# Attention scores on 64 array rows instead of 32 in the mixer of a four-layer network, with its second q and k projected midway

## The chip, the cores and the metric

The kernel runs on one core of a Trainium2 chip. The metric is the device time of one execution in microseconds (us), the median of several runs. Before the change it is 6611.78 us, the median of three runs (6609.2, 6611.78 and 6629.58 us). The profile is of one further execution, whose span is 6630.4 us.

## The reference

Eight images of 256 channels and 32 x 32 = 1024 positions go through four residual layers, each fed by a group norm of the current x. Everything is float32.

```python
x = x + _L0_conv_ref(_gn(x), ...)   # attention over 1024 positions, 8 heads of 64
x = x + _L1_conv_ref(_gn(x), ...)   # 3x3 convolution
x = x + _L2_conv_ref(_gn(x), ...)   # 3x3 convolution
x = x + _L3_conv_ref(_gn(x), ...)   # selective scans, gates, then a mixer, then a 3x3 depthwise step
```

The change is in layer 3, in the part that the code calls the mixer. Its input is xm2, 1024 positions of 256 channels:

```python
x_local = conv1d(xm2.transpose(0, 2, 1), lc_w, lc_b, groups=Cc, pad=1).transpose(0, 2, 1)
x_global = mha(xm2, attn_inw, attn_inb, attn_outw, attn_outb)   # 8 heads of 32
x_out = jnp.concatenate([x_local, x_global], axis=-1) @ fc_w.T + fc_b
...
att = jax.nn.softmax(q @ k.transpose(0, 1, 3, 2) * (1.0 / hd ** 0.5), axis=-1)   # hd = 32
```

## The kernel before

**Stages of an image.** front_attention is layer 0 and front_convs are layers 1 and 2. scan_layers holds the norms and the selective scans of layer 3 in four branches. back_layers holds the gates, the projections and the mixer; back_out and back_end hold the projections, norms and the depthwise convolution behind it, up to the output.

**Order of the work.** Everything is written out without loops on the chip. For each image b, interleave (line 1335) mixes two streams. The dense stream has the back layers of image b-1 (its mixer is in it), then the front of image b+1. The other stream is the scans of image b. Each piece of the dense stream yields a cost; a step of the scans is placed each time the sum of the costs has grown by PACE (line 1364: 1.8 for the first image, 2.95 for the middle ones, 1.6 for the last). So the places of the scans among the dense instructions follow from the yielded costs alone. Each engine runs its own queue in order, and an instruction that waits holds up all that is behind it. In the mixer of image 6 the scans of image 7 run alongside and no front follows; the mixer of image 7 runs with nothing beside it.

**Scans.** A unit of scans goes drive (GpSimd multiplies du by bc into hs, line 931), decays (ScalarE, da), scan (VectorE, hs), weigh (GpSimd, line 963) and add_up (TensorE sums into y, four matmuls at once with sel, 128 rows by 32 columns).

**The mixer** (mixer_attention, line 1044). v is projected for all heads. Then q and k are projected, 256 channels each, as two tiles of 128 channels for each: a tile holds four heads of 32 rows. All four projections come before the attention, in the order q of heads 0 to 3, k of heads 0 to 3, q of heads 4 to 7, k of heads 4 to 7. The evacuation from the PSUM adds the bias and, for q, multiplies by 32^-0.5, on VectorE.

**The attention loop** (attention) is shared by the front and the mixer. It takes pairs of heads. A unit is one pair, one half of the 1024 queries and one block of 128 keys; there are 64 units. A unit's scores are two matmuls, one for each head, into the two halves of one 1024-column PSUM tile, big, of which there are two; k is the stationary operand. ScalarE takes the exponential of it into p. Two units later, values multiplies p by v, again two matmuls, each with 128 rows and 64 columns, into acc. In the front a head has 64 channels, so the two scores of a pair use array rows 0 to 63 and 64 to 127. In the mixer a head has 32, so they use two neighbouring strips of 32 rows (0 and 32, or 64 and 96). A float32 matmul shows as two instructions in the profile, so the scores of a unit are four and the values four.

A pair's tensors are asked for 8 units before its first unit (pair_of(units[n + 8]["t"])). When a pair is done, take copies acc out, and DMAs carry the outputs and the sums of the exponentials to o and to a DRAM tile; after the second pair of a q tile, invert divides by the sums.

**Shared tiles.** work() gives tiles of 128 x 1026 from a pool of 12 (tp). q, k, o, p, x2 (the mixer's input), local and most other temporaries of the dense stream come from it, and each waits until one is free.

**local.** Before mixer_attention starts, back_layers computes x_local for both channel tiles (depthwise3: one ScalarE and two VectorE operations for each). The loop around the mixer counts its yields; at the 58th it makes the first statistics and the norm of the next image's front (next(begin)).

The engine proxies (line 101) issue nearly all instructions, so nearly all groups of the profile have line 101 and are told apart by their tiles: big<-qk,qk are the mixer's scores, big<-q,k the front's, acc<-p,v the values of both.

Of the kernel before, what the change touches and what calls it, by code (L numbers as in the profile page):

```python
# [19 lines left out]
P = 128  # L20
# [13 lines left out]
def preact_stack(ctx: ExitStack, tc: tile.TileContext, I, out, cols):  # L34
# [28 lines left out]
    def work(name):  # L63
        return tp.tile([P, TP], F32, tag="t", name=name)
# [4 lines left out]
    def big_tile():  # L69
        return ps_big.tile([P, N], F32, tag="big", name="big")  # L70
# [142 lines left out]
    vector.tensor_scalar_mul(qdw, qdw, 2.0)  # L213
    half_d = wp.tile([P, NB], F32, name="half_d")
    vector.tensor_scalar_mul(half_d, vec[:, cols["mD"] : cols["mD"] + NB], 0.5)
    half_qb = wp.tile([P, 2], F32, name="half_qb")
    vector.tensor_scalar_mul(
        half_qb, vec[:, cols["qpwb"] : cols["qpwb"] + 2], 0.5
# [140 lines left out]
    def inner(t):  # L359
        return t[:, 1 : N + 1]  # L360
# [683 lines left out]
    def mixer_attention(x2, img, exact=False):  # L1044


        v = vp.tile([P, NKT, 8, 64], F32, tag="v", name="v3")
        vector.memset(v[:, :, :, 32:64], 1.0)
        wv = chunk("ainv", 0)
        for kt in range(0, NKT, 4):  # L1050
            ps = big_tile()
            for i in range(4):
                for c in range(2):
                    tensor.matmul(
                        ps[:, i * C : (i + 1) * C],
                        inner(x2[c])[:, (kt + i) * P : (kt + i + 1) * P],
                        wv[:, c],
                        start=c == 0,
                        stop=c == 1,
                    )  # L1060
            vector.tensor_copy(
                v[:, kt : kt + 4, :, 0:32],
                ps.rearrange("p (k a b) -> p k a b", k=4, b=32),
            )
            yield 3.8

        qk = {}
        for t in (0, 2, 1, 3):
            qk[t] = work("qk3")
            w = chunk("ainqk", t)  # L1070
            ps = big_tile()
            for h in range(2):
                for c in range(2):
                    tensor.matmul(
                        ps[:, HALVES[h]],
                        w[:, c],
                        inner(x2[c])[:, HALVES[h]],
                        start=c == 0,
                        stop=c == 1,
                    )  # L1080
            scale = 32.0**-0.5 if t < 2 else 1.0
            vector.tensor_scalar(
                qk[t][:, 0:N], ps, col("ain_b", t), scale, ALU.add, ALU.mult
            )
            yield 3.4

        o = img["o3"] = [work("o3_0"), work("o3_1")]

        def head(i):
            t, rows = i // 4, slice((i % 4) * 32, (i % 4) * 32 + 32)  # L1090

            def take(half, acc):

                vector.tensor_scalar_add(
                    o[t][rows, half], acc, col("ain_b", 4 + t, rows)
                )

            return {
                "q": qk[t][rows, 0:N],
                "k": qk[2 + t][rows, 0:N],  # L1100
                "v": lambda kt: v[:, kt, i, 0:32],
                "rows": rows,
                "take": take,
            }

        if exact:
            attention_exact(head(i) for i in range(8))
            return

        sums = {}  # L1110

        def pair(i):
            t = i // 4
            rows = [slice((j % 4) * 32, (j % 4) * 32 + 32) for j in (i, i + 1)]

            def v_of(j):
                return lambda kt: v[:, kt, j]

            def take(h, acc, _):
                if t not in sums:  # L1120
                    sums[t] = dp.tile([4, N], F32, tag="sums4", name="sums")
                both = half_work("both")
                scalar.copy(both, acc)
                for e in range(2):
                    j, at = (i + e) % 4, e * 64
                    nc.sync.dma_start(
                        out=o[t][rows[e], HALVES[h]], in_=both[at : at + 32]
                    )
                    nc.sync.dma_start(
                        out=sums[t][j : j + 1, HALVES[h]],  # L1130
                        in_=both[at + 32 : at + 33],
                    )
                if i % 4 == 2 and h == 1:
                    ot = o[t][:, 0:N]

                    def finish(r):
                        vector.tensor_mul(ot, ot, r)
                        vector.tensor_scalar_add(ot, ot, col("ain_b", 4 + t))

                    return invert(sums[t], 4, 32, finish)  # L1140

            return {
                "q": [qk[t][r, 0:N] for r in rows],
                "k": [qk[2 + t][r, 0:N] for r in rows],
                "v": [v_of(i), v_of(i + 1)],
                "take": take,
            }

        yield from attention([lambda i=i: pair(i) for i in range(0, 8, 2)], False)

    def back_layers(img, exact=False, begin=None):

# [64 lines left out]
        for t in x2:  # L1217
            zero_ends(t)

        def evac_x2(m, ps):  # L1220
            vector.scalar_tensor_tensor(
                inner(x2[m]), ps, col("fpw_b", m), inner(xs[m]), ALU.add, ALU.add
            )

        yield from project("fpw", fd, evac_x2)


        local = [work("local0"), work("local1")]
        for t in range(2):
            depthwise3(local[t][:, 0:N], x2[t], "lc_w", "lc_b", t)  # L1230
        for n, cost in enumerate(mixer_attention(x2, img, exact)):
            yield cost
            if n == 58 and begin is not None:
                next(begin)
        img["mix"] = xt, local

    def back_out(img):
# [89 lines left out]
    def drain(*streams):  # L1327
        for s in streams:
            for _ in s:
                pass  # L1330
# [200 lines left out]
```

## Time and profile before

| What | Value |
|---|---|
| Median of 3 runs | 6611.78 us |
| Span of the profiled execution | 6630.4 us |
| TensorE (PE) busy | 5708.6 us, 86% |
| VectorE (DVE) busy | 3903.6 us, 59% |
| ScalarE (ACT) busy | 2687.2 us, 41% |
| GpSimd (POOL) busy | 2684.8 us, 40% |
| Mean granted TensorE clock | 0.892 of full |
| Mixer's scores, big<-qk,qk, 32 rows, 2048 instructions | 658.2 us busy |
| Front's scores, big<-q,k, 64 rows, 2048 instructions | 602.5 us busy |
| Values of both, acc<-p,v, 4096 instructions | 1189.7 us busy |
| Mixer of image 0 to 5, first score to last | 181.7 to 191.0 us |
| Mixer of image 6 (beside the last scans), mixer of image 7 (alone) | 349.7 us, 130.1 us |

A group's line in the profile reads: line, engine, operation, the tiles out<-in with their shapes, the count; then busy microseconds and mean nanoseconds of one; then idle time of the engine just before, and what ended most of it. Matmuls overlap, so the mean of one is longer than busy time divided by the count. PEclk is the clock granted to TensorE as a share of full speed[...]. "Chain" is the chain of waits that ended last. The seven mixers with scans beside them are longer than the one that runs alone.

### The profile page before, as it was taken

The page shows a single profiled execution, that of the slowest core. Times are in us where ns is not written, and L with a number is a line of the kernel's source. Part 1 is how long each engine was busy: PE and PEld are TensorE (multiplying, and loading weights), DVE is VectorE, ACT ScalarE, POOL GpSimd, SP SyncE. Part 2 cuts the span into 40 slices and gives each one's busy share as a digit, 9 for nine tenths or more (in the row PEclk, how much of TensorE's full clock was granted, in tenths as well). Part 3 has the DMA queues.
Part 4 walks back from the last instruction along what each step waited for, and adds up shares of the span by engine and source line. Part 5 has one row for each costly group of instructions (what it writes and reads, how often), then busy time and mean ns, then how long its engine had stood idle before and what let it go on. Part 6 is the DMA issues. An engine that isn't in the chain of part 4 may idle for free.

```text
span 6630.4 us, 52730 instructions
## 1 busy us (share of the span) xinstructions
PE 5708.6 (86%) x17602; PEld 1926.6 (29%) x17602; DVE 3903.6 (59%) x4613; ACT 2687.2 (41%) x3225; POOL 2684.8 (40%) x1295
## 2 busy tenths in 40 slices
PE   8887689897998979998899989999799988978596
PEld 2331133222422234222332223222342223311222
DVE  4248745577465775567655675557755676455522
ACT  4134424553254532544245432555235442344242
POOL 0016662634355251642526334462526426176300
PEclk9988888998998989899999989899899999867697
DMA  1022332322233122331223222241213212233200
GB/s 41 27 60 79 77 90 73 101 60 65 74 97 91 48 69 76 88 83 52 76 78 92 70 64 80 72 110 45 79 59 105 79 53 80 65 94 89 58 21 26
DMA packets 217969, 471.36 MB, mean 71 GB/s; under 512 B 60244, under 2 KB 103636, under 8 KB 215640
## 3 DMA queue, kind: packets, MB, share of 16 engines
q1 hardware_dynamic: 217688, 467.90, 25.4%
q8 instruction: 141, 2.31, 0.1%
q14 instruction: 140, 1.15, 0.1%
HBM read 395.36 MB, written 63.96 MB: 69 GB/s over the span
## 4 chain that ended last, share of the span: by engine, by line
PE 53%; DVE 25%; DMA 6%; issue 6%; ACT 5%; POOL 4%; SPq 1%; POOLq 0%; DVEq 0%; ACTq 0%
PE big L101 34%; PE acc L101 12%; DVE hs L101 5%; PE da L101 4%; DVE p L101 3%; PE y L101 2%; DVE u L101 2%; DVE dw L101 2%; POOL hs L963 2%; POOL hs L931 2%; DVE t L101 1%; DVE dt L101 1%; DMA du_m<-a 1%; DVE st L101 1%; ACT p L101 1%
## 5 line engine op out<-in xcount | busy, mean ns | idle before, releaser
L931 POOL TENSOR_TENSOR hs<-du,bc 128x1024 f32<-128x1024 f32 x512 | 1319.8, 2594 | 1912.6 <-DMA du<-du_m 767.4
L963 POOL TENSOR_TENSOR hs<-hs,bc 128x1024 f32<-128x1024 f32 x512 | 1278.8, 2498 | 693.2 <-DVE hs L101 480.4
L101 ACT ACTIVATE p<-big 128x1024 f32<-128x1024 f32 x1024 | 1036.1, 1019 | 769.3 <-PE big L101 764.8
L101 PE MATMUL acc<-p,v 128*64 128x512 f32 x4096 | 1189.7, 653 | 2.6 <-ACT o L101 2.6
L101 PE MATMUL big<-im,w 128*128 128x512 f32 x2304 | 1073.7, 622 | 120.9 <-ACT im L101 102.6
L101 ACT ACTIVATE da<-dt,a_neg 128x512 f32<-128x512 f32 x1024 | 688.7, 687 | 791.3 <-DVE hs L101 484.3
L101 DVE TENSOR_TENSOR p<-p 128x1024 f32<-128x1024 f32 x448 | 717.0, 1600 | 273.7 <-ACT p L101 183.9
L101 DVE TENSOR_TENSOR_SCAN hs<-da,carry,hs 128x512 f32<-128x512 f32 x512 | 628.2, 1268 | 382.8 <-POOL hs L931 301.2
L101 DVE TENSOR_TENSOR_SCAN hs<-da,hs 128x512 f32<-128x512 f32 x512 | 600.0, 1207 | 256.8 <-ACT da L101 166.3
L101 PE MATMUL big<-q,k 64*128 64x512 f32 x2048 | 602.5, 657 | 76.7 <-ACT p L101 47.8
L101 PE MATMUL big<-qk,qk 32*128 32x512 f32 x2048 | 658.2, 687 | 9.2 <-ACT p L101 6.5
L101 PEld LDWEIGHTS big<-im,w 128*128 128x128 f32 x2304 | 445.4, 198 | 752.0 <-issue 613.8
L101 PE MATMUL y<-hs,sel 128*32 128x512 f32 x2048 | 410.9, 676 | 210.9 <-POOL hs L963 180.8
L962 POOL COPY carry<-hs 128x2 f32<-128x2 f32 x256 | 97.5, 381 | 947.6 <-DVE hs L101 928.2
L101 PEld LDWEIGHTS acc<-p,v 128*64 128x64 f32 x4096 | 217.6, 140 | 843.2 <-issue 759.8
L101 PEld LDWEIGHTS big<-qk,qk 32*128 32x128 f32 x2048 | 173.8, 195 | 487.2 <-issue 269.2
L101 PEld LDWEIGHTS big<-q,k 64*128 64x128 f32 x2048 | 161.2, 188 | 503.0 <-issue 247.4
L101 PE MATMUL big<-o,w 128*128 128x512 f32 x384 | 196.2, 664 | 92.6 <-DVE o L101 92.6
L101 PE MATMUL big<-xn,w 128*128 128x512 f32 x512 | 232.4, 608 | 5.6 <-ACT p L101 5.6
L101 DVE SCALAR_TENSOR_TENSOR dw<-xo,vec,dw 128x961 f32<-128x961 f32 (+1 forms) x128 | 194.1, 1550 | 29.3 <-ACT dw L101 29.1
L101 DVE SCALAR_TENSOR_TENSOR u<-raw,vec,u 128x1024 f32<-128x1024 f32 x96 | 153.9, 1603 | 87.2 <-ACT u L101 86.7
L101 DVE SCALAR_TENSOR_TENSOR xt<-big,vec,xt 128x1024 f32<-128x1024 f32 x48 | 61.4, 1279 | 236.2 <-PE big L101 236.2
(191 smaller groups left out, 5231.1 us busy)
## 6 DMA issues: line engine op xcount, KB each, us to landing
bc<-bc SPq DMA_DIRECT2D x1024, 128.0 KB
dt<-dt_m SPq DMA_DIRECT2D x512, 128.0 KB
du<-du_m SPq DMA_DIRECT2D x512, 128.0 KB
w<-in_wc SPq DMA_DIRECT2D x192, 192.0 KB
rs<-inv SPq DMA_DIRECT2D x64, 256.0 KB
dt_m<-dt SPq DMA_DIRECT2D x64, 256.0 KB
du_m<-a SPq DMA_DIRECT2D x64, 256.0 KB
xt<-in_x SPq DMA_DIRECT2D x8, 1024.0 KB
```

The lines of the kernel that those rows point to most:

```text
L101: made = issue(*args, **kwargs)
L931: nc.gpsimd.tensor_mul(u["hs"], u["du"], both_groups(u["bc"][:, 0]))
L962: nc.gpsimd.tensor_copy(carry[:, u["q"], g : g + 2], hs[:, :, HALF - 1])
L963: nc.gpsimd.tensor_mul(hs, hs, both_groups(u["bc"][:, 1]))
```

## The change

Each head's scores are to use 64 rows of the array. The pair becomes heads i and i + 2 of one q tile, which lie in different halves of the 128 rows. k is taken in those halves, 64 rows with the channels of two heads. So that the second head in the half adds nothing, q is kept twice: once with heads 1 and 3 set to zero, once with heads 0 and 2. A column of factors, alt, that is 32^-0.5 or 0 by strips of 32 rows makes both in the evacuation: VectorE makes the first, ScalarE the second, with a bias that is already multiplied (alt_b). This is the arrangement in which the array sees as many rows as in the front.

Two more things move. A second q takes more of the shared tiles, so q and k of heads 4 to 7 are projected when their first pair is asked for (unit 24), in a drain that yields no cost to the pace of the scans, and no longer ahead of the attention. And local is computed midway, after the 34th and the 40th yield, instead of before; the norm of the next front stays at the same unit (yield 56 instead of 58, as two yields are gone). The branch marked exact is adapted; it runs only when the sums are out of range.

```diff
+    alt = wp.tile([P, 2], F32, name="alt")
+    nc.gpsimd.memset(alt, 0.0)
+    for g in range(4):
+        nc.gpsimd.memset(alt[g * 32 : g * 32 + 32, g % 2 : g % 2 + 1], 32.0**-0.5)
+    alt_b = wp.tile([P, 2, 2], F32, name="alt_b")
+    for t in range(2):
+        vector.tensor_scalar_mul(alt_b[:, t], alt, col("ain_b", t))
...
         qk = {}
-        for t in (0, 2, 1, 3):
-            qk[t] = work("qk3")
-            w = chunk("ainqk", t)
-            ps = big_tile()
...
-            scale = 32.0**-0.5 if t < 2 else 1.0
-            vector.tensor_scalar(
-                qk[t][:, 0:N], ps, col("ain_b", t), scale, ALU.add, ALU.mult
-            )
-            yield 3.4
+
+        def q_and_k(t):
+            for at in (t, 2 + t):
+                w = chunk("ainqk", at)
+                ps = big_tile()
...
+                if at == t:
+                    q = [work("qk3")[:, 0:N] for _ in range(2)]
+                    vector.tensor_scalar(
+                        q[0], ps, col("ain_b", t), alt[:, 0:1], ALU.add, ALU.mult
+                    )
+                    scalar.activation(
+                        q[1], ps, AF.Identity, bias=alt_b[:, t, 1:2], scale=alt[:, 1:2]
+                    )
+                else:
+                    k = work("qk3")[:, 0:N]
+                    vector.tensor_scalar_add(k, ps, col("ain_b", at))
+                yield 3.4
+            qk[t] = q, k
+
+        yield from q_and_k(0)
...
         def pair(i):
             t = i // 4
-            rows = [slice((j % 4) * 32, (j % 4) * 32 + 32) for j in (i, i + 1)]
+            if t not in qk:
+                drain(q_and_k(t))
+            q, k = qk[t][0][i % 2], qk[t][1]
...
                 for e in range(2):
-                    j, at = (i + e) % 4, e * 64
+                    j, at = i % 4 + 2 * e, e * 64
...
-                if i % 4 == 2 and h == 1:
+                if i % 4 == 1 and h == 1:
...
             return {
-                "q": [qk[t][r, 0:N] for r in rows],
-                "k": [qk[2 + t][r, 0:N] for r in rows],
-                "v": [v_of(i), v_of(i + 1)],
+                "q": [q[e * 64 : e * 64 + 64] for e in range(2)],
+                "k": [k[e * 64 : e * 64 + 64] for e in range(2)],
+                "v": [v_of(i), v_of(i + 2)],
                 "take": take,
             }
 
-        yield from attention([lambda i=i: pair(i) for i in range(0, 8, 2)], False)
+        yield from attention([lambda i=i: pair(i) for i in (0, 1, 4, 5)], False)
...
-        local = [work("local0"), work("local1")]
-        for t in range(2):
+        local = []
+
+        def add_local():
+            t = len(local)
+            local.append(work("local"))
             depthwise3(local[t][:, 0:N], x2[t], "lc_w", "lc_b", t)
+
         for n, cost in enumerate(mixer_attention(x2, img, exact)):
             yield cost
-            if n == 58 and begin is not None:
+            if n in (34, 40):
+                add_local()
+            if n == 56 and begin is not None:
                 next(begin)
+        while len(local) < 2:
+            add_local()
         img["mix"] = xt, local
```

More of the change, by code (lines that the diff above doesn't have):

```diff
@@ L1067, in mixer_attention @@
         qk = {}
-        for t in (0, 2, 1, 3):
-            qk[t] = work("qk3")
-            w = chunk("ainqk", t)
-            ps = big_tile()
[L1072 to L1079, printed above, removed]
-                    )
-            scale = 32.0**-0.5 if t < 2 else 1.0
-            vector.tensor_scalar(
-                qk[t][:, 0:N], ps, col("ain_b", t), scale, ALU.add, ALU.mult
-            )
-            yield 3.4
+        def q_and_k(t):
+            for at in (t, 2 + t):
+                w = chunk("ainqk", at)
+                ps = big_tile()
+                for h in range(2):
+                    for c in range(2):
+                        tensor.matmul(
+                            ps[:, HALVES[h]],
+                            w[:, c],
+                            inner(x2[c])[:, HALVES[h]],
+                            start=c == 0,
+                            stop=c == 1,
+                        )
[3 more added lines that the diff above has]
+                        q[0], ps, col("ain_b", t), alt[:, 0:1], ALU.add, ALU.mult
+                    )
+                    scalar.activation(
[7 more added lines that the diff above has]
+        yield from q_and_k(0)
         o = img["o3"] = [work("o3_0"), work("o3_1")]
@@ L1096, in take @@
                 )
+            if t not in qk:
+                drain(q_and_k(t))
             return {
-                "q": qk[t][rows, 0:N],
-                "k": qk[2 + t][rows, 0:N],
+                "q": qk[t][0][i % 2][rows],
+                "k": qk[t][1][rows],
                 "v": lambda kt: v[:, kt, i, 0:32],
@@ L1113, in pair @@
             t = i // 4
-            rows = [slice((j % 4) * 32, (j % 4) * 32 + 32) for j in (i, i + 1)]
+            if t not in qk:
+                drain(q_and_k(t))
+            q, k = qk[t][0][i % 2], qk[t][1]
             def v_of(j):
@@ L1124, in take @@
                 for e in range(2):
-                    j, at = (i + e) % 4, e * 64
+                    j, at = i % 4 + 2 * e, e * 64
                     nc.sync.dma_start(
-                        out=o[t][rows[e], HALVES[h]], in_=both[at : at + 32]
+                        out=o[t][j * 32 : j * 32 + 32, HALVES[h]],
+                        in_=both[at : at + 32],
                     )
```

## The prediction

> **What bounds the kernel now.** I read the page first: which engine is busiest, at what clock it ran, and which chain ended last.
>
> ```profile
> PE 5708.6 (86%) x17602; PEld 1926.6 (29%) x17602; DVE 3903.6 (59%) x4613; ACT 2687.2 (41%) x3225; POOL 2684.8 (40%) x1295
> ...
> PEclk9988888998998989899999989899899999867697
> ...
> PE 53%; DVE 25%; DMA 6%; issue 6%; ACT 5%; POOL 4%; SPq 1%; POOLq 0%; DVEq 0%; ACTq 0%
> ```
>
> TensorE is busy 86% of the span and holds 53% of the chain; its clock is not always full (mean 0.892 in the view of cores). So a TensorE microsecond counts, and so does the clock at which it is spent. Next, the groups of instructions that the change touches, from the page:
>
> ```profile
> L101 PE MATMUL acc<-p,v 128*64 128x512 f32 x4096 | 1189.7, 653 | 2.6 <-ACT o L101 2.6
> ...
> L101 PE MATMUL big<-q,k 64*128 64x512 f32 x2048 | 602.5, 657 | 76.7 <-ACT p L101 47.8
> L101 PE MATMUL big<-qk,qk 32*128 32x512 f32 x2048 | 658.2, 687 | 9.2 <-ACT p L101 6.5
> ```
>
> The front attention scores with 64 rows (q,k), the mixer with 32 (qk,qk), with the same number of instructions. The mixer's cost 56 us more. Is a 32-row pair slower in itself? The timeline of TensorE in undisturbed stretches, mixer of the last image, then front of the first (start, us, what):
>
> ```profile
> 6420.72 1.13 PE L101 MATMUL big<-qk,qk 32*128 32x512 f32 x4
> 6421.77 1.08 PE L101 MATMUL acc<-p,v 128*64 128x512 f32 x4
> 6422.78 1.13 PE L101 MATMUL big<-qk,qk 32*128 32x512 f32 x4
> ```
> ```profile
> 164.58 1.13 PE L101 MATMUL big<-q,k 64*128 64x512 f32 x4
> 165.64 1.08 PE L101 MATMUL acc<-p,v 128*64 128x512 f32 x4
> 166.65 1.13 PE L101 MATMUL big<-q,k 64*128 64x512 f32 x4
> ```
>
> No: one unit of scores and values takes 2.06 to 2.07 us in both. The difference is the clock. Windows over whole stages (mixers of images 1, 6 and 7, then the front of image 3; stretch, length, PE busy, PEclk, DMA share, GB/s):
>
> ```profile
> 1868.20:2058.10 189.90, 173.92 (x625) 0.90 0.35 92
> 5759.50:6109.20 349.70, 279.19 (x737) 0.72 0.32 84
> 6366.70:6496.80 130.10, 129.78 (x505) 1.00 0.05 13
> 2124.00:2301.30 177.30, 170.66 (x629) 0.99 0.21 56
> ```
>
> The trace's clock is only ever 1.00 or 0.50 and changes on a grid of 3.413 us. Windows on that grid, three in the mixer of image 6, two in the front of image 1:
>
> ```profile
> 5771.51:5774.93 3.42, 3.42 (x10) 0.50 0.20 52
> 5774.93:5778.34 3.41, 3.41 (x8) 0.50 0.27 102
> 5778.34:5781.75 3.41, 3.41 (x10) 0.50 0.00 0
> 487.73:491.14 3.41, 3.41 (x6) 0.50 0.02 4
> 491.14:494.55 3.41, 3.41 (x16) 1.00 0.27 73
> ```
>
> Both times TensorE is fully busy at half clock. In the front one such window brings the full clock back; in the mixer it stays at half for ten windows (5764.7 to 5798.8). I counted this over the whole trace, weighing matmul time in each window by the rows in use over 128 (a pair of 32-row scores is 64/128, a pair of 64-row ones and the values 128/128). Of the half-clock windows with TensorE 97% busy, 0 of 55 between 0.70 and 0.80 were followed by full clock, 6 of 11 between 0.80 and 0.90, and 85 of 107 above (the other 22 hold one-column matmuls, acc or da<-mean_w,ln_sq). Going down: below 0.45 all 112 full-clock windows were followed by half, above 0.55 7 of some 1,365. The mixer's steady alternation is (64+128)/2 = 96 rows, 0.75: it can keep a full clock but never win it back. With 64 rows it is 1.0.
>
> [...]
>
> **The change part by part.**
> - Scores: 2048 instructions before and after, at equal cadence: 0. Weight loads 195 to 188 ns, hidden behind matmuls: 0.
> - Clock, the main term. A busy half-clock window that follows another busy half-clock window, neither with the low-row da<-low or da<-xn,w_minw ahead, is a stuck one: in the eight mixers I count 4, 4, 4, 4, 13, 4, 24 and 0 of them (57), in the eight fronts none. A stuck window does 3.413 x 0.5 = 1.71 us less work than it could. Image 4's 13 look like bad luck of this execution (6630.4 us against a median of 6611.8), so I count 4: 48 x 1.71 = 82 us. In images 0 to 5 (24 windows, 41 us) the chain of waits runs through PE in these windows, so I take 0.8: 33 us. In image 6 (24, 41 us) it returns to the scans (DVE and POOL hs hold 26% of the chain there), so 0.7: 29 us. About five of the 27 drops to half start at an activity of 0.38 to 0.51 that 64 rows lift past the bound; I take three avoided at 2 windows: 10 us. Sum 72 us. Bounds: 0, if rows that hold zeros don't count, to 120.
> - q twice: per half of the heads, one DVE evacuation as before (1284 ns; a column for the scale instead of a constant), and one ACT evacuation more. Nearest row: glob<-big 128x1024, 1113 ns. 16 x 1.1 = 18 us on ACT (41% busy), behind attention: the copy is first read by the second pair, 16 units or 33 us later. 0 on the path.
> - Second q, k: two projections of 3.43 us each (in the last image's timeline their evacuations qk<-big start 3.43 us apart: 6356.55, 6359.98, 6363.41) move from ahead of attention to unit 24, and stand there in PE's queue ahead of the scores. They need both big buffers, whose release waits for the DVE evacuation, which can stand in DVE's queue behind a scan (2.3 us the pair) that waits for POOL. Fronts do the same three times each and idle 177.3 - 170.7 = 6.6 us in all, so 2 us each; under heavy scans the wait before such an evacuation was up to 5 us (629.1 to 634.3). I take 3 us x 8 = +24.
> - local: 4 DVE operations x 1283 ns and 2 ACT x 1241 ns leave the start of the mixer, where DVE's queue holds them ahead of the a and v that the scans and values wait for (5.1 us of DVE), and come back at units 30 and 36, beside matmuls. At the start TensorE waits for the first scans (6.6 us before y at 1891 in image 1). PE arrives 7 us earlier, but the scans, placed by summed dense costs, come 6.8/2.1 = 3 units later in its queue, so the gap shrinks by up to 5 us. I take 3 us x 8 = -24. In their new place they delay scans on DVE by 2.6 us each time; the unpaced 7 us of projection gives the scans that slack.
> - Buffers: of 12 shared tiles, 9 or 10 are held at units 24 to 33 (x2 2, q and k 6, o 1 or 2), which leaves 2 or 3 for p instead of 4 or 5. With three nothing waits; with two the exponential waits for the values two units back, about 1 us, inside its slack. 0, at worst 5 us an image.
> - alt and alt_b: small setup while x is loaded (DVE idles 0.9 us before it at 8.7): 0. The exact branch isn't run.
>
> Sum: -72 + 24 - 24 = -72: 6611.8 - 72 = 6540 us.
>
> **The rivals.**
> - [...] the moving rows with zero q count as idle. The clock stays, the moves cancel or cost: 6611.8 + 0 to 24, say 6620. For it: no stream of zeros is in the trace to test it. Against it: windows full of y<-hs,sel with a one-hot sel, of da<-u,w_moutw (64 columns) or da<-u,w_mxpw (36 columns) restore the clock, so it is not the useful work that is counted. Chance 0.12.
> - The mid-attention projections bring a new wait: 5 us of evacuation plus a new drop to half clock (an idle window, then one busy at half, 1.7 to 3.4 us), with the held buffers 5 us, some 12 us x 8 = 96, against 72 won: 6636, slower. For it: idle of 4 to 6 us by the projections of the front of image 1 (450.8, 637.7). Against it: the steady fronts lose 2 us each. Chance 0.10.
> - More drops avoided and all of the stuck windows on the path: -120 with the local move: 6490. For it: PE has the most of the chain in the mixers. Against it: scans take over in image 6. Chance 0.15.
>
> **How the numbers follow.** The main case has 0.63 and gives 6540, with 6510 to 6585 for its own unknowns. The range, 6480 to 6605, takes in the third rival and the upper side of the main case, and leaves out the first two, 0.22 in all. Faster by 0.3% means below 6592: the main case and the third, with the share of the middle taken off, 0.83; same 0.08, mostly the first rival; slower 0.09, the second and a part of the first.
>
> **What would show it.** The windows over the six middle mixers should have PEclk 0.95 or more (0.90 before), image 6's 0.80 or more, with stretches of half clock of one or two busy windows, never ten. Score pairs should keep 1.06 us. The glob-like ACT evacuation should be 1.1 us and hold nobody. It is wrong if half-clock runs stay long in the mixers (first rival), or if TensorE idles at unit 24 of each mixer behind the evacuation of q or k (second).

## The result, and the profile after

The changed kernel takes 6821.27 us (median of four runs, 6820.28 to 6823.8) against 6620.68 us before (four runs, 6609.2 to 6635.23). The ratio is 1.0302, with a 95% interval of 1.0278 to 1.0327: 200 us slower, where 72 us faster was predicted. The profiled spans are 6822.1 and 6630.4 us.

The page of the kernel after, busy times and granted clock:

```profile
PE 5667.2 (83%) x17602; PEld 1924.3 (28%) x17602; DVE 4037.0 (59%) x4615; ACT 2710.6 (40%) x3241; POOL 2740.4 (40%) x1300
...
PEclk9988798997999979998899988999889997978697
```

TensorE has 41 us less busy time than before (5708.6), though the span grew by 192 us. So, in sum, the new time is idle time of TensorE, not slower matmuls. Its groups of scores and values, from the same page:

```profile
L101 PE MATMUL acc<-p,v 128*64 128x512 f32 x4096 | 1163.2, 639 | 2.9 <-ACT both L101 2.3
...
L101 PE MATMUL big<-q,k 64*128 64x512 f32 x2048 | 607.8, 670 | 119.4 <-ACT big L101 76.0
L101 PE MATMUL big<-qk,qk 64*128 64x512 f32 x2048 | 638.1, 672 | 45.9 <-ACT p L101 34.0
```

The mixer's scores, now 64*128, cost 20 us less than before (658.2), and the values 27 us less. The front's scores, which the diff doesn't touch, have 119.4 us of idle time ahead of them, against 76.7 before. Windows of the kernel after over the stages shown for before (mixers of images 1, 6 and 7, front of image 3; stretch, length, PE busy, PEclk, DMA share, GB/s):

```profile
1906.70:2105.20 198.50, 176.75 (x640) 0.91 0.34 91
5968.90:6306.60 337.70, 253.57 (x752) 0.81 0.34 90
6551.60:6688.80 137.20, 136.88 (x520) 1.00 0.05 15
2172.70:2362.50 189.80, 172.72 (x625) 0.96 0.20 51
```

Image 6's clock went from 0.72 to 0.81, and its mixer from 349.7 to 337.7 us: here the change did what it is for. Image 7's longer stretch only has the second projections inside it now. But the front of image 3 is 12.5 us longer, at 0.96 instead of 0.99. By the same reading the convolutions (images 2 to 7) went from 200 to 203.5 us to 215 to 217 us, and the fronts from 177.3 to between 189.8 and 192.5. From the start of one mixer to the start of the next the kernel after takes 36 us longer (mean of the six such stretches, images 0 to 6). The front gives 14 of them, the convolutions 14, the stretch between the two 4, the way from the mixer to the front 2. The mixer, with what leads into it, gives 1. The loss is in stages that the diff doesn't touch.

In the convolutions the clock fell as well. Those of image 3, before and after (two windows, each of its own kernel):

```profile
2359.00:2563.00 204.00, 181.96 (x486) 0.91 0.28 79
2424.70:2641.80 217.10, 183.45 (x494) 0.88 0.26 78
```

In the convolutions of images 2 to 7 the half clock lasts 51 to 54 us each, against 30 to 37 before.

What TensorE waits for, in the view of its waits (engine, line waited for: us in total, times, longest). Three of its lines, before:

```profile
PE big L101 <- ACT im L101: 102.6, 16, 10.6
PE da L101 <- DVE hs L101: 76.6, 28, 7.4
PE big L101 <- ACT big L101: 17.6, 23, 1.7
```

After:

```profile
PE da L101 <- DVE hs L101: 177.6, 37, 11.2
PE big L101 <- ACT im L101: 157.7, 16, 15.9
PE big L101 <- ACT big L101: 76.0, 23, 8.1
```

The first belongs for the most part to the mixer's start (below). The second is the first matmul of each convolution, which waits for the im tiles from ScalarE; the third is the front's scores behind a projection of q and k. The second and third grew by 113 us with the same count of instructions. The third, in the timeline of the kernel after, at the third projection in the front of image 3 (start, us, what, and in brackets the wait):

```profile
2282.17 7.82 DVE L101 TENSOR_TENSOR p<-p 128x1024 f32<-128x1024 f32 x3
2284.95 7.13 PE L101 MATMUL big<-xn,w 128*128 128x512 f32 x16
2293.76 1.22 DVE L101 TENSOR_TENSOR o<-o,rs 128x1024 f32<-128x1024 f32 x1 [3.76 <-DMA rs<-inv]
2294.90 1.22 DVE L101 TENSOR_TENSOR p<-p 128x1024 f32<-128x1024 f32 x1
2296.04 2.60 DVE L101 SCALAR_TENSOR_TENSOR u<-raw,vec,u 128x1024 f32<-128x1024 f32 x2
2298.55 1.22 DVE L101 COPY q<-big 128x1024 f32<-128x1024 f32 x1
2299.86 1.01 ACT L101 ACTIVATE big<-big 128x1024 f32<-128x1024 f32 x1 [12.47 <-DVE q L101]
2301.03 1.23 PE L101 MATMUL big<-q,k 64*128 64x512 f32 x2 [7.95 <-ACT big L101]
```

The projection ran from 2284.95 to 2292; its evacuation stood in VectorE's queue behind three p<-p (7.8 us), a wait for a DMA and two operations of a scan branch (u), and ran at 2298.55, 13.6 us after the projection's start. ScalarE waited 12.5 us and TensorE 8 us. In the front of image 3 before, q is copied 4.1 us after the projection's start, while its second half still runs:

```profile
2237.43 7.13 PE L101 MATMUL big<-xn,w 128*128 128x512 f32 x16
2239.26 2.33 DVE L101 TENSOR_TENSOR_SCAN hs<-da,hs 128x512 f32<-128x512 f32 x2
2241.51 1.20 DVE L101 COPY q<-big 128x1024 f32<-128x1024 f32 x1
```

In all fronts of before the same wait is at most 1.7 us. VectorE's p<-p, which the diff doesn't touch, took 780.5 us in all after and 717.0 before.

**Where the scans stand.** The order within TensorE's queue can be read from the trace: how many units (four score matmuls, or four matmuls of a convolution) go ahead of each group of y<-hs,sel, the last step of a unit of scans. I counted it for the front and the convolutions of image 3 and the mixer ahead of them (the scan sums come in pairs, one number for each pair):

| Kernel | mixer, from unit 13 on | front, of 64 units | first convolutions, in fours of matmuls |
|---|---|---|---|
| before | 15, 21, 26, 32, 37 ... | 11, 27, 43, 59 | 6, 9, 15, 21, 27 ... (22 groups) |
| after | 13, 18, 24, 29, 35 ... | 4, 20, 36, 52 | 3, 6, 12, 18, 24 ... (24 groups) |

In the mixer the steps moved three units, as the prediction has it (its first groups went from 4, 8, 9, 10 to 7, 10, 13, 13; so 10 became 13 and 15 became 18). In the front they stand seven units earlier. Both have one cause. The second projections go through drain, so their two yields of 3.4 are lost, 6.8 of dense cost for each image. In the mixer a unit yields 2.1, and 6.8 are three units. Behind the mixer, the same sum of costs is reached 6.8 later, so a given *sum* belongs to a later dense instruction for the rest of the image: in the front, whose costs are scaled by 0.35 (SLOW, line 1363 of the kernel before), 6.8 are 6.8 / 0.735 = 9 units. The steps repeat every 16 units there, so 9 units later is 7 units earlier for the next one: 11 became 20 and 4. A front asks for its next projection 8 units ahead of the pair, at units 8, 24 and 40. The scan steps now stand four units ahead of these, where they stood three behind.

### The profile page after: what moved, and what is told of

The parts are those of the page before. It is cut to its first block, busy times and chain, and to the rows that moved or that the text cites. A ratio compares the mean times of both kernels' runs of the same rounds, so it can differ in the third digit from the quotient of the medians.

```text
span 6822.1 us, 52762 instructions
## 1 busy us (share of the span) xinstructions
PE 5667.2 (83%) x17602; PEld 1924.3 (28%) x17602; DVE 4037.0 (59%) x4615; ACT 2710.6 (40%) x3241; POOL 2740.4 (40%) x1300
## 5 line engine op out<-in xcount | busy, mean ns | idle before, releaser
L971 POOL TENSOR_TENSOR hs<-hs,bc 128x1024 f32<-128x1024 f32 x512 | 1305.1, 2550 | 815.1 <-DVE hs L101 687.4
L101 PE MATMUL big<-im,w 128*128 128x512 f32 x2304 | 1085.4, 628 | 174.6 <-ACT im L101 157.7
L101 PE MATMUL acc<-p,v 128*64 128x512 f32 x4096 | 1163.2, 639 | 2.9 <-ACT both L101 2.3
L101 DVE TENSOR_TENSOR p<-p 128x1024 f32<-128x1024 f32 x448 | 780.5, 1742 | 355.6 <-ACT p L101 284.3
L101 PE MATMUL big<-q,k 64*128 64x512 f32 x2048 | 607.8, 670 | 119.4 <-ACT big L101 76.0
L101 PE MATMUL big<-qk,qk 64*128 64x512 f32 x2048 | 638.1, 672 | 45.9 <-ACT p L101 34.0
L970 POOL COPY carry<-hs 128x2 f32<-128x2 f32 x256 | 123.1, 481 | 1288.1 <-DVE hs L101 1209.3
L101 PE MATMUL y<-hs,sel 128*32 128x512 f32 x2048 | 380.0, 661 | 180.3 <-POOL hs L971 180.2
L101 PE MATMUL big<-o,w 128*128 128x512 f32 x384 | 221.0, 732 | 132.8 <-DVE o L101 105.3
L101 PEld LDWEIGHTS big<-qk,qk 64*128 64x128 f32 x2048 | 173.0, 193 | 493.6 <-issue 277.3
L101 DVE SCALAR_TENSOR_TENSOR dw<-xo,vec,dw 128x961 f32<-128x961 f32 (+1 forms) x128 | 222.4, 1767 | 30.5 <-ACT dw L101 29.1
L101 PE MATMUL da<-xn,w_minw 64*128 64x512 f32 x256 | 149.4, 699 | 45.8 <-DVE hs L101 45.6
```

Source lines behind the costliest of these rows:

```text
L101: made = issue(*args, **kwargs)
L970: nc.gpsimd.tensor_copy(carry[:, u["q"], g : g + 2], hs[:, :, HALF - 1])
L971: nc.gpsimd.tensor_mul(hs, hs, both_groups(u["bc"][:, 1]))
```

## The experiments

Two theories were to be told apart. P, the pace: the lost 6.8 of cost moves the scans' places behind the mixer, and that is the loss. Its rival: the moved instructions themselves, q and k at unit 24 or local at units 30 and 36, bring new waits. A third question is whether the clock gain of the 64 rows is there at all. Each time below is a median, beside the kernel before on the same chip: 6619.28 us for the first group (the cost lost, the cost given back at the first q and k, the 64 rows alone, the second q and k ahead), 6624.94 for the second (the cost given back behind the mixer, before with local midway, VectorE operations added, scans earlier), 6627.77 for the rest. A difference between kernels of two groups carries the few us by which these differ.

**Before with the cost lost, and nothing else.**

```diff
-            yield 3.4
+            yield 3.4 if t % 2 == 0 else 0.0
```

> The kernel before with one number different: the yields of the third and fourth of the mixer's q and k projections give 0 instead of 3.4. Nothing is computed elsewhere; only the scan steps come 6.8 of cost later in the order. P: slower by most of the loss, 6760 to 6830. M and R: no change beyond 20 us, 6590 to 6640.

6879.79 us, ratio 1.0386 [1.0359, 1.0413], 50 us above the expected stretch: 260 us slower without any instruction added, removed or resized. Its scan steps stand at 4, 20, 36, 52 in the front and at 3, 6, 12 in the convolutions, exactly as after. Its fronts took 189 to 192 us, its convolutions 212 to 217. Its waits are those of the kernel after in the two lines that the fronts and convolutions carry:

```profile
PE big L101 <- ACT im L101: 155.5, 16, 15.9
PE da L101 <- DVE hs L101: 104.0, 30, 9.4
PE big L101 <- ACT big L101: 75.5, 23, 8.1
```

Outside the mixers this kernel loses as much as the kernel after. Summed from the mixer of image 0 to that of image 6, it is 269 us longer than before, and 205 of them lie in the fronts, the convolutions and the stretches behind the mixer and between the two. The other 64 lie in the mixers, still on 32 rows. Their half clock lasts 48 to 89 us each, against 31 to 58 before. Its mixers of images 1 and 3:

```profile
1918.10:2110.10 192.00, 176.61 (x625) 0.88 0.31 86
3556.60:3764.50 207.90, 197.68 (x625) 0.79 0.28 79
```

**After with the cost given back behind the mixer.**

```diff
         yield from attention([lambda i=i: pair(i) for i in (0, 1, 4, 5)], False)
+        yield 6.8
```

> The changed kernel with 6.8 of cost yielded once, behind the last unit of the mixer: inside the mixer the scan steps stand as in the changed kernel, behind it (front, convolutions) as before. If the loss by the missing cost lies behind the mixer (the changed kernel's fronts are 13 to 16 us and its convolutions 12 to 15 us longer there): fronts 176 to 178 us and convolutions 200 to 203 us again, mixers 192 to 199 us, in all 6590 to 6660 us. If it lies inside the mixer: 6750 to 6820.

6607.01 us, 0.9973 [0.9963, 0.9984], so 214 us below the kernel after. The places in the front and the convolutions are those of before again (11, 27, 43, 59), those in the mixer remain as after. Fronts took 176 to 178 us, convolutions 200 to 203.5. Its waits:

```profile
PE da L101 <- DVE hs L101: 149.4, 36, 11.2
PE big L101 <- ACT im L101: 102.4, 16, 10.6
PE big L101 <- ACT big L101: 16.4, 24, 1.5
```

The second and third lines are back at the values of before. P is shown from both sides, and so is where it acts. VectorE's p<-p is back as well, at 716.9 us.

**After with the cost given back at the first q and k.** The two projections ahead yield 6.8 each.

```diff
-                yield 3.4
+                yield 6.8
```

> The changed kernel with one number different: each of the two yields of the first q and k gives 6.8 instead of 3.4, so that the mixer's summed cost is again what it was before and each scan step stands again at its old place among the dense stages behind the mixer. Theory P (pace): the 200 us come from the 6.8 of cost that the drained projections no longer yield; the front yields at 0.35, so scan steps stand some 9 attention units later there. Then this returns to 6540 to 6640 us. Theory M (moves): the loss is the projection at unit 24 and local at units 30 and 36, which are all still here: 6780 to 6830. Theory R (rows): the second q and its evacuation on ScalarE cost it: 6780 to 6830.

6656.25 us, 1.0052 [1.0032, 1.0072], 16 us above the expected stretch: 165 us of the 214 come back. Fronts and convolutions have the places of before, so what lacks is lost in the mixers (200 to 206 us, against 192 to 199 with the cost behind the mixer).

**The 64 rows alone.** Both projections ahead, local as before.

```diff
         yield from q_and_k(0)
+        yield from q_and_k(1)
...
-            if n in (34, 40):
-                add_local()
-            if n == 56 and begin is not None:
+            if n == 58 and begin is not None:
```

(and local's block of the kernel before in the place of add_local)

> The kernel before with the 64 rows alone: q twice and pairs two heads apart, but all projections and local ahead of the attention as before, same yields. Clock theory of the prediction: half-clock stretches in the mixers of one or two busy windows, mixer of image 6 some 30 us shorter, in all 6530 to 6580. P: same side, since the pace is unchanged. R: 6780 to 6830.

6551.52 us, 0.9895 [0.9872, 0.9918]: 68 us faster than before, and the best kernel of this study. Windows of this kernel over mixers of images 1, 6 and 7 and the front of image 3:

```profile
1869.80:2048.10 178.30, 164.78 (x624) 0.95 0.35 95
5718.70:6040.50 321.80, 245.23 (x737) 0.81 0.34 91
6294.40:6424.50 130.10, 129.78 (x505) 1.00 0.05 13
2114.20:2289.90 175.70, 169.08 (x629) 1.00 0.20 56
```

The mixers that run beside scans are 3 to 12 us shorter in images 1 to 5 (181.7 to 191.0 before, 178.3 to 183.2 here), and 28 us in image 6; the one that runs alone is unchanged at 130.1 us. Of the stuck half-clock windows that the prediction counts (57 in the mixers of before) 3 are left, and also 3 in the kernel after. Of the half-clock windows in the mixers with TensorE busy throughout, those with the low-row da<-low or da<-xn,w_minw left out, 31 of 34 were followed by full clock, against 25 of 82 before. The 12 shared tiles were enough with both projections ahead, so the second q alone did not call for the midway projection.

**Pairs two heads apart, but 32 rows.** The control for the rows: the kernel before with the new order of heads.

```diff
-            rows = [slice((j % 4) * 32, (j % 4) * 32 + 32) for j in (i, i + 1)]
+            rows = [slice((j % 4) * 32, (j % 4) * 32 + 32) for j in (i, i + 2)]
...
-        yield from attention([lambda i=i: pair(i) for i in range(0, 8, 2)], False)
+        yield from attention([lambda i=i: pair(i) for i in (0, 1, 4, 5)], False)
```

> A control: the kernel before with pairs two heads apart, but each head on its 32 rows with one q (strips 0 and 64, or 32 and 96). Row theory: only the rows that move count for the clock, so half-clock runs in the mixers stay long and the time is that of before, 6600 to 6640. If the distance of the two strips in the array were what restores the clock: 6540 to 6570.

6653.86 us, 1.0046 [1.0028, 1.0065], 14 us above the expected stretch. Windows of its mixers of images 1 and 6:

```profile
1876.50:2065.20 188.70, 172.86 (x625) 0.91 0.35 93
5781.50:6128.40 346.90, 270.47 (x737) 0.74 0.32 84
```

The clock is close to that of before (0.90 and 0.72), 59 windows are stuck, and 26 of 85 busy half-clock windows recover. So the gain in the clock comes with the rows, zeros included, and not with the distance of the heads. Where its own 26 us come from was not followed.

**Second q and k ahead, local midway.**

```diff
         yield from q_and_k(0)
+        yield from q_and_k(1)
...
-            if n in (34, 40):
+            if n in (36, 42):
```

> The changed kernel with the second q and k projected ahead of the attention again, each with its yield of 3.4 (the yields of local and of the next front are counted two later, so they stay at the same units). P: the cost is back too, so 6540 to 6640, about as with the cost alone. M, if the projection at unit 24 is at fault: the same 6540 to 6640; if local midway is: 6780 to 6830. R: 6780 to 6830. Together with the run that gives only the cost back this tells P from M.

6634.21 us, 1.0023 [1.0012, 1.0034]. Its scans have the places of before everywhere, and it differs from the 64 rows alone only in local: moving local costs 83 us. The timeline of this kernel at the second local of image 1:

```profile
1981.22 6.40 DVE L101 SCALAR_TENSOR_TENSOR local<-x,vec,local 128x1024 f32<-128x1024 f32 x2 [0.48 <-ACT local L101]
1987.74 2.16 ACT L101 ACTIVATE p<-big 128x1024 f32<-128x1024 f32 x2 [1.86 <-DVE local L101]
...
1999.55 1.22 PE L101 MATMUL da<-xn,w_minw 64*128 64x512 f32 x1 [4.58 <-DVE hs L101]
```

Two operations that took 1283 ns each where they stood before hold VectorE for 6.4 us here, beside scans and GpSimd. An exponential waits for local, and some 10 us later TensorE waits 4.6 us for a scan. From unit 24 on, in the mixers of images 0 to 5 together, such waits of da for hs come to 32.6 us, against 10.2 in the 64 rows alone. That local's time on VectorE makes them is read from the trace only.

**Before with local midway.** The rival's other half, without the 64 rows and without the lost cost.

```diff
-        local = [work("local0"), work("local1")]
-        for t in range(2):
+        local = []
+        def add_local(): ...
...
+            if n in (36, 42):
+                add_local()
```

> The kernel before (32 rows, projections ahead, all yields as before) with local alone computed at units 30 and 36. With 64 rows this move cost 6634 - 6552 = 83 us. If it is a cost of its own: 6680 to 6720. If it needs the tiles of the second q to hurt (three more of the 12 shared tiles): 6600 to 6640.

6700.64 us, 1.0119 [1.0091, 1.0147]: 76 us, near the 83.

**The 64 rows alone, with VectorE operations added.** Two operations of local's kind, written at each of the two places of local midway; they compute max(t x 1, t), so they add time and leave the values as they are.

```diff
+            if n in (36, 42):
+                t = local[n // 42][:, 0:N]
+                for _ in range(2):
+                    vector.scalar_tensor_tensor(t, t, 1.0, t, ALU.mult, ALU.max)
```

> The kernel with the 64 rows alone (local ahead), and at units 30 and 36 two VectorE operations of local's size on local itself, which leave its values as they are; no ScalarE work, no other tile. Theory V (VectorE time): what local costs midway is its 4 x 1.28 us in VectorE's queue among the scans: 6600 to 6640. Theory B (buffers): what costs is that x2 holds shared tiles and p waits for local: 6540 to 6570.

6597.1 us, 0.9957 [0.9942, 0.9971], 46 us above the 64 rows alone. But the operations don't run where the edit writes them. In all eight mixers the trace has them ahead of the first score, at the start of the mixer. Those of image 1, whose first score comes at 1870.02:

```profile
1841.99 1.22 DVE L101 SCALAR_TENSOR_TENSOR local<-local 128x1024 f32<-128x1024 f32 x1
1845.46 1.22 DVE L101 SCALAR_TENSOR_TENSOR local<-local 128x1024 f32<-128x1024 f32 x1
1854.65 2.47 DVE L101 SCALAR_TENSOR_TENSOR local<-local 128x1024 f32<-128x1024 f32 x2
```

So this run says nothing of VectorE's time at units 30 and 36, and neither of its two theories is tested. It shows that 4.9 us more of VectorE at the mixer's start cost 46 us. Which part of local's 83 us is VectorE's time, the ScalarE operation or the later tiles stays open.

**The 64 rows alone, scans earlier.** All four projections yield 5.1 instead of 3.4, so the sum has 6.8 more instead of 6.8 less.

```diff
-                yield 3.4
+                yield 5.1
```

> The kernel with the 64 rows alone, its four q and k projections yielding 5.1 instead of 3.4, so the scan steps behind them come 6.8 of cost earlier than before, the opposite of what the change did. If the cost is a delay that can only hurt, earlier scans give the same or better: 6500 to 6560. If what counts is which scan step falls on which dense stage (chance of a collision), anything from 6500 to 6800, and the fronts or the convolutions should differ from the 176 and 200 us that they have with the 3.4.

6728.79 us, 1.0152 [1.0128, 1.0176], 177 us above the 64 rows alone. So the loss is no matter of the scans coming late. The stages tell it apart. The front's steps stand at 1, 17, 34, 50 here and its fronts take 177 to 180 us, hardly longer than before; TensorE waits 32.6 us behind their projections, not 76. The convolutions' steps start at 3, 6, 12, as after, and take 209 to 210 us, but the wait for im is 108.1 us, not 157.7: their places alone don't make that wait. Here TensorE waits for mv, VectorE's means and variances, 82.4 us in all against 11.3 before. The mixer's steps stand three units earlier than before (12 for 15), and the mixers of images 0 to 5 take 198 to 203 us, 22 us more each than in the 64 rows alone; this is most of the loss. Their half clock lasts 31 to 48 us, against 17 to 27.

**After with local ahead and the cost given back.** This leaves the 64 rows and the midway projection.

```diff
         yield from attention([lambda i=i: pair(i) for i in (0, 1, 4, 5)], False)
+        yield 6.8
...
-            if n in (34, 40):
-                add_local()
```

(and local's block of before)

> The changed kernel with local ahead of the attention again and 6.8 of cost yielded behind the mixer: what stays of the change is the 64 rows and the second q and k projected at unit 24. Against the run with the cost at the end (6607 us) local midway goes: if its cost adds to the rest (76 to 83 us in the two runs that had it or left it out alone), 6525 to 6550. If the tiles run short instead (x2, local, the first q and k and then the second hold 10 or 11 of 12 at unit 24), p waits there: mixers longer than 185 us and 6590 to 6660.

6592.76 us, 0.9944 [0.9925, 0.9963]. Local midway costs only 14 us here (6607.01 - 6592.76). The time lies in the stretch expected for short tiles, and the mixers take 193 to 196 us. But behind unit 24, where the tiles are fullest, TensorE idles less than in the next kernel, which has all projections ahead (28.5 against 41.3 us, table below), so short tiles are not what the trace shows.

**The 64 rows alone, with the second projections ahead but their cost behind.** From unit 13 of the mixer on, the scans stand as in the kernel just shown; only the place of the projections differs.

```diff
-        yield from q_and_k(1)
+        drain(q_and_k(1))
...
+        yield 6.8
```

> The kernel with the 64 rows alone (6552 us), all projections ahead, but the second q and k yield nothing and 6.8 is yielded behind the mixer: only the scan steps beside the mixer's units come later, those behind it stand as before. If later scans beside the mixer are what made the changed kernel with the cost at the end 49 us faster than with the cost at the first q and k: 6500 to 6540. If each place is a matter of collisions: 6540 to 6650, with mixers of 180 to 195 us.

6556.47 us, 0.9897 [0.9873, 0.9921]. Three units of shift inside the mixer alone cost nothing that can be told from the 64 rows alone (5 us). With 32 rows the same places of the scans went with 11 us more in each mixer (before with the cost lost). The midway projection costs 36 (6592.76 - 6556.47). Where it acts is the mixer's start. In the timelines of image 1, first of the kernel after, then of before:

```profile
1937.22 1.08 PE L101 MATMUL acc<-p,v 128*64 128x512 f32 x4
1949.51 2.77 PE L101 MATMUL da<-u,w_mxpw 128*36 128x512 f32 x3 [11.21 <-DVE hs L101]
```

```profile
1891.22 1.92 PE L101 MATMUL y<-hs,sel 128*32 128x512 f32 x4 [6.59 <-POOL hs L963]
```

TensorE comes to the first scans with 7 us less to do, and waits for longer (11.2 us against 6.6). In the kernel with local ahead and the projection midway another wait comes first, at unit 2 of image 1:

```profile
1875.28 1.28 ACT L101 ACT_TABLE_LOAD   x1 [6.29 <-DMA dt<-dt_m]
...
1877.81 1.92 ACT L101 ACTIVATE p<-big 128x1024 f32<-128x1024 f32 x2
1878.87 2.08 PE L101 MATMUL big<-qk,qk 64*128 64x512 f32 x4 [5.61 <-ACT p L101]
```

The first exponentials stand in ScalarE's queue behind the first decays and their table load (1.28 us), which wait 6.3 us for the DMA of dt; TensorE then waits 5.6 us. With all projections ahead TensorE is still projecting when dt lands: in the 64 rows alone the table load starts at 1866.06, behind the same DMA, and the projections of image 1 run from 1853.49 to 1867.49. I summed TensorE's idle stretches above 0.1 us over the mixers of images 0 to 5, from 20 us ahead of the first score on:

| Kernel | median us | idle up to unit 24 | idle later |
|---|---|---|---|
| before | 6620 to 6628 | 37.3 | 38.5 |
| 64 rows alone | 6551.5 | 53.3 | 36.4 |
| the same, second cost behind | 6556.5 | 59.4 | 41.3 |
| local ahead, projection midway | 6592.8 | 108.0 | 28.5 |
| projection ahead, local midway | 6634.2 | 53.0 | 75.4 |
| after, cost behind | 6607.0 | 104.5 | 35.0 |
| after | 6821.3 | 105.1 | 32.9 |

Projecting midway (local ahead) adds 48.6 us up to unit 24, 33.7 of them at unit 2, and takes 12.8 off later: 35.8 us, against 36 in the time. Local midway adds 39 us later on where the scans have the places of before, and 6.5 where they stand three units later.

## Why the prediction was wrong

**The step that failed** is in the part on local: "PE arrives 7 us earlier, but the scans, placed by summed dense costs, come 6.8/2.1 = 3 units later in its queue, so the gap shrinks by up to 5 us." The lost 6.8 of cost was seen, sized and then followed to the end of the mixer only, as a small help; behind the mixer it was put at nothing. It carries on through the front and the convolutions of the same image, where the same 6.8 are nine units and not three. There it puts a scan branch's VectorE work ahead of q's evacuation (76.0 us of waits against 17.6), and lengthens the wait for the first im tiles of the convolutions (157.7 against 102.6); both stages also run longer at half clock. It measured +165 us (cost given back at the first q and k) to +214 (behind the mixer), and +260 on the kernel before, where the mixers lose too. With the places of before in the fronts and convolutions the change is a little faster than before, by 0.3%.

Point by point:

- **Clock of the 64 rows, predicted -72: -68.** Right in mechanism and size (the 64 rows alone), with 57 stuck windows down to 3. By parts, it won 28 us in image 6 (29 predicted) and 43 from the mixer of image 0 to that of image 6 (33 and 10). The middle mixers' PEclk of 0.95, named as a sign, is there with the 64 rows alone; in the kernel after, image 1 has 0.91. The gain is also in the kernel after, in image 6 (337.7 against 349.7 us) and in TensorE's busy time. What hides it: new half-clock time after the new waits, 14 to 20 us in each front against 3 and 51 to 54 in the convolutions against 30 to 37. So the mean clock fell to 0.888 from 0.892 though only 3 stuck windows were left in the mixers. The rival that rows with zeros don't count falls: with half of each q zero, 3 stuck windows of 57 are left, and the control with 32 rows has 59. The windows that the prediction set against it are three in the kernel before, each filled to 99% or more of its matmul time by one of da<-u,w_mxpw (637.91), da<-u,w_moutw (2429.91) and y<-hs,sel (3126.23), and each followed by full clock.
- **Score pairs at 1.06 us, q twice at nothing:** the costs held, the place of the copy did not quite. The VectorE evacuation took 1344 ns (1284 before), the ScalarE copy 1203 ns (1.1 us estimated). But with both projections ahead the second copy stands behind the first decays in ScalarE's queue, and the first score waits for it, 15.3 us in all (PE big <- ACT qk); the 68 us are net of this.
- **Second q and k midway, +24: +22 to +36** (22 from the kernel with projection ahead to the one with the cost at the first q and k; 36 where only their place differs). The sum is about right, the reason is not. The prediction put the cost at unit 24, in the wait for an evacuation. It is at the start: the second projections had filled time in which TensorE would otherwise wait for the first decays and scans.
- **Local midway, -24: +14 to +83.** Wrong in sign. In image 1 the first unit of scans (its drive on GpSimd) began only 1.5 us earlier, measured from the evacuation of x2 (30.15 us after it with local ahead, 28.6 midway), not 3 to 5: less of VectorE's 5.1 us stood in its way than the step assumes. "The unpaced 7 us of projection gives the scans that slack" fits the 14 us, measured with that projection midway, against 76 and 83 without it; the scans' places differ as well, so the slack isn't shown by itself.
- **The second rival**, new waits by the midway projection (6636), named the right kind of loss in the wrong place. No rival followed the cost past the mixer; the range had no case for it. The chance of 0.83 for faster is also more than its own cases give, 0.63 and 0.15.

Taken one after the other, the terms are -68 (rows), +83 (local), +22 (projection), +165 (cost), in all +202. Along another path local is worth 14 and the cost 214, so the terms depend on each other. That local costs 83 or 14 could come from its place relative to the scan steps, which stand at 26 and 32 in one kernel and at 29 and 35 in the other, with local at 30 and 36 in both; local's four operations take about 9 us of VectorE in each. This is argued only. Why the cost given back at the first q and k is 49 us worse than behind the mixer stays open as well; the loss lies in the mixers (about 204 us against 196), though TensorE's idle time, summed as in the table, is nearly the same (143 us against 140), and later scans beside the mixer alone made no such difference (5 us).

What the change is for can be had without its loss: the 64 rows with both projections and local ahead, all yields kept, beat both kernels at 6551.52 us.

## What to carry to other kernels

Where a written-out order is placed by summed costs, a yield that is dropped, moved or added is a change to everything behind it: compare the order of the queues over a whole period before costing the instructions themselves. Time gained by moving work away from the start of a stage is only gained if TensorE isn't waiting there for something else (here the projection midway added 48.6 us of idle time up to unit 24, and the kernel became 36 us slower). When the array clock hangs at half in a busy stretch, look at how many rows the matmuls use (here 64 rows in place of 32 left 3 stuck windows of 57). And before a run with an added instruction is read, see in its trace where that instruction ran.

## What the runs showed of the hardware

- Whether a busy stretch gets the full clock back went with the rows in use, and rows that hold zeros counted. With q zero in every other strip of 32 rows, 31 of 34 busy half-clock windows in the mixers were followed by full clock (the 64 rows alone); with 32 rows, and the heads as far apart, 26 of 85, and in the kernel before 25 of 82. So in these mixers a busy window alone wasn't enough. Three windows of the kernel after in the mixer of image 6 (same columns):

```profile
5973.46:5976.87 3.41, 1.98 (x4) 0.51 0.95 250
5976.87:5980.28 3.41, 3.41 (x10) 0.50 1.04 233
5980.28:5983.69 3.41, 3.41 (x13) 0.99 0.33 71
```

  One half-clock window that is busy throughout, then full clock, where the kernel before stayed at half for ten.
- Half-clock time came with waits: in the fronts of the kernel after, with 8 us waits behind projections, it grew from 3 us to 14 to 20 us in each, without any change to their matmuls, and in the convolutions from 30 to 37 us to 51 to 54.
- At half clock the same matmuls took 1.8 times as long. In the mixers of before, the four instructions of a unit's scores took 2.08 us and those of its values 1.98 us at a PEclk of 0.50 (image 6, from 5771.69), and 1.13 and 1.08 us at 1.00 (image 7, from 6420.72); a unit came every 3.91 us against 2.06. From these two I estimate that a stuck window does 3.413 x (1 - 2.06/3.91) = 1.6 us less work; the prediction took 1.71.
- The same two VectorE operations took 1.28 us each in one place (local's, mean of the kernel before) and 3.2 us each (6.40 us the two) beside GpSimd multiplies, in the second local of image 1 of the kernel with projection ahead and local midway. Such a time is not the rule there: the median of its 32 operations on local is 1.33 us.
